# A post-norm block on one Trainium2 core: first values and one head's exponentials issued in pieces, and another order at the end

## The chip, the cores and the metric

The kernel runs on one core of a Trainium2 chip. The metric is the device time of one execution in microseconds (us); a time for a kernel is the median of its runs. Profiles are of one execution each, with their own time.

The engines are named as in the profile: PE (TensorE, matrix products; PEld is its loading of weights), DVE (VectorE), ACT (ScalarE), POOL (GpSimd) and SP (SyncE, which here only issues DMAs).

## The reference

The input x has 32 sequences of 512 tokens with 256 features. There are 16 heads of 16 features. Each sequence goes through a double causal attention, a residual and a layer norm; then the 512 tokens of the first sequence go through a mixture of 8 experts (the router's choices and weights cover 512 tokens), and everything is normed a second time. Cut to what matters:

```python
qk = x @ W_attn + b_attn                      # q and k; the values are x itself
y  = causal_attn(q, k, v)                     # first attention, softmax over keys
e  = v[:, :, 1:] - y[:, :, :-1]               # what the first one missed, one token on
k2 = x[:, :-1] @ W_k2 + b_k2
y2 = causal_attn(q[:, :, 1:], k2, e)          # second attention, with a zero row in front
x  = layernorm(x + proj(y) + proj(y2))
x  = layernorm(x + experts(x))                # in the kernel: experts for sequence 0 only
```

## The kernel before, in words

**Groups and steps.** A group is 4 heads of one sequence; there are 32 x 4 = 128 groups (`n_all`). `step(n)` runs for n = 0 to 131. In one step the kernel works on several groups at once: the maxima of group n, the exponentials of groups n - 1 and n - 2, the values (products of probabilities and values) of group n - 2, and the projections for groups to come. A step has five **slots** (`slot(n, u)`, u = 0 to 4), each followed by a **gap**, whose work stands in a list `rest[u]`. `add(gap, f, ...)` appends to such a list; some calls insert at its head. The order on PE, SP, DVE and POOL is the order of the Python calls; ACT's order is the scheduler's.

**A slot** makes scores twice: `maxima` (L271) multiplies queries and keys to find each row's maximum (PE products L301 and a mask L286, then DVE's `tensor_reduce`, L325), and `scores` (L356) makes the turned scores, minus the maximum (PE, L372), takes the exponential on ACT (L384) and sets what lies above the diagonal to zero on POOL (L388). Both are done for two pairs of heads; pair 1's scores are issued first, then pair 0's. Each head of a pair has its own PSUM bank. The tile of a slot has one or two **parts**, listed in `banks` (L348): slots 0 and 2 have parts of 384 and 128 columns, slot 3 has two of 256, slots 1 and 4 have one of 512. A part is three products for each head: two for queries and keys, and one for the maxima (`m_t`, `minus`).

**PSUM.** `pair_of_banks` (two buffers of two banks) holds the maxima's scores; `bank` (L81, four buffers of one bank) serves everything else: the turned scores (four for each slot), projections (`pj`), values (`av`), transposes (`yt`), the output projection (`po`), the experts. A product that takes a new buffer waits until the buffer taken four allocations earlier has been read.

**Values.** `values(n, a, lo, hi)` (L428) multiplies probabilities `pt` and values: `v_pad` for the first attention (a = 0), `e_pad` for the second (a = 1). Each product fills 32 rows for one of 4 heads, over the columns from its key block on. A copy by ACT (L450) takes the result to SBUF (`avs`). For a = 0 it is one call over 512 columns, in gap 1; for a = 1 there are two calls, columns 0 to 255 in gap 3 and 256 to 511 in gap 4. `normalize` (L499) turns the first attention's result on PE (`yt`), divides it and makes `e_pad` on DVE and POOL.

**Sums.** Two groups share a tile (`packed[two]`). `gather` (L452) sends softmax sums to DRAM and numerators to a packed tile; `narrow` (L464) loads the sums of both attentions back as 128 x 64, `inverse` (L469) inverts them on DVE, `unload` (L474) writes them to DRAM, `widen` (L479) loads them spread over the heads' rows (two DMAs of 256 KB), `weigh` (L487) multiplies (DVE, L490), and `unite` (L492) adds the two attentions on POOL (L497) into `ysT`. For the last two groups `narrow` to `unite` stand in step 130, and `attended` in step 131.

**Output.** `attended` (L543) makes four blocks of 128 tokens: products with W_proj (`po`, L551), the residual's addition on DVE (L554), then `twice_normed` (L560) with statistics (L566, L567). `scaled` (L573) makes the factor on POOL (L577, L578) and applies it: on POOL for most sequences, on DVE for the last one, followed by the store. For sequences 1 to 30 `scaled` is issued one gap after `attended`; for the last sequence `twice_normed` calls it at once, for each block.

Of the kernel before, what the change touches and what calls it, by code (L numbers as in the profile page):

```python
# [9 lines left out]
F32 = mybir.dt.float32  # L10
# [3 lines left out]
AF = mybir.ActivationFunctionType  # L14
# [3 lines left out]
P = 128  # L18
HD = 16
HS = 32  # L20
GH = 4
NH2 = 2
RUN = 64
# [12 lines left out]
def half(ap):  # L36
    return ap.bitcast(F32R)
# [3 lines left out]
def block_kernel(  # L41
# [16 lines left out]
    nc = tc.nc  # L58
    B, T, C = x.shape
    NB = T // P  # L60
    NC = C // P
# [10 lines left out]
    work = ctx.enter_context(tc.tile_pool(name="work", bufs=2))  # L72
    small = ctx.enter_context(tc.tile_pool(name="small", bufs=4))
    psum = ctx.enter_context(tc.tile_pool(name="psum", bufs=1, space=bass.MemoryType.PSUM))
    dram = ctx.enter_context(tc.tile_pool(name="dram", bufs=2, space=bass.MemoryType.DRAM))
# [13 lines left out]
    seqs = {}  # L89
# [109 lines left out]
    packed = {}  # L199
    moments = {}  # L200
# [155 lines left out]
    def scores(n, u, pair):  # L356
        parts = [p for p in banks[u] if 0 <= n - p[3] < n_all]
        if not parts:
            return [], lambda: None
        ps = [bank(f"sc{n}_{u}_{pair}_{hh}") for hh in range(NH2)]  # L360
        pt = work.tile([P, NH2, T], F32, tag=f"pt{u}", name=f"pt{n}_{u}_{pair}", bufs=2)
        todo = []


        def score(d, a, j, at, k, hh, rows):
            keys = minus[a][rows] if k == 2 else d["kk"][rows, a, j * P : (j + 1) * P]
            queries = d["q"][rows, k, j * P :] if k < 2 else d["m"][rows]
            to = ps[hh][:, at * P : at * P + T - j * P]
            if k == 2:
                queries = queries.rearrange("p (r i q) -> p i r q", r=GH, i=NB)[:, j:]  # L370
                to = to.rearrange("p (i r q) -> p i r q", r=GH, q=HS)
            nc.tensor.matmul(to, half(keys), half(queries), start=(k == 0), stop=(k == 2))  # L372

        for a, j, at, lag in parts:
            d = groups[n - lag]
            d["pt", a, j, pair] = pt[:, :, at * P : at * P + T - j * P]
            for k in range(3):
                todo.append((T - j * P, partial(score, d, a, j, at, k)))

        def exponentials():  # L380
            lo = parts[0][2] * P
            hi = parts[-1][2] * P + T - parts[-1][1] * P
            for hh in range(NH2):
                nc.scalar.activation(pt[:, hh, lo:hi], ps[hh][:, lo:hi], AF.Exp, scale=HD**-0.5)  # L384

            for a, j, at, _ in parts:
                diag = pt[:, :, at * P : (at + 1) * P]
                nc.gpsimd.affine_select(  # L388
                    diag, diag, pattern=[[0, NH2], [1, P]], compare_op=ALU.is_ge, fill=0.0, base=-a,
                    channel_multiplier=-1,  # L390
                )

        return todo, exponentials
# [34 lines left out]
    def values(n, a, lo=0, hi=T):  # L428
        b, g = divmod(n, NG)
        d = groups[n]  # L430
        vals = (v_pad, e_pad)[a]

        def first_of(g, h):
            return (g // 2 * GH + h) * WIDE + 2 * (g % 2)

        ps = bank(f"av{n}_{a}_{lo}")
        order = [j for j in ([0, 2, 1, 3] if a == 0 else [0, 1, 3, 2]) if j * P < hi]
        for j in order:
            first = max(lo, j * P)
            for h in range(GH):  # L440
                nc.tensor.matmul(  # L441
                    ps[HS * h : HS * (h + 1), first - lo : hi - lo],
                    vals[:, j, first_of(g, h) : first_of(g, h) + HS],
                    d["pt", a, j, h // NH2][:, h % NH2, first - j * P : hi - j * P],
                    start=(j == order[0]),
                    stop=(j == order[-1]),
                )
        if lo == 0:
            d["avs", a] = work.tile([P, T], F32, tag="avs", name=f"avs{n}_{a}")
        nc.scalar.copy(d["avs", a][:, lo:hi], ps[:, 0 : hi - lo])  # L450

# [9 lines left out]
        nc.sync.dma_start(p["sums"][a, k], avs[(HS - 1) * k :: HS])  # L461
        nc.sync.dma_start(p[a][GH * HD * k : GH * HD * (k + 1)], avs[1 - k :: 2])

    def narrow(two):  # L464
        p = packed[two]
        t = p["den"] = small.tile([P, RUN], F32, tag="den", name=f"den{two}", bufs=1)
        nc.sync.dma_start(t, p["sums"].rearrange("a k h (c q) -> (a k h c) q", q=RUN))

    def inverse(two):  # L469
        t = packed[two]["den"]  # L470
        nc.vector.tensor_scalar_max(t, t, 1e-30)
        nc.vector.reciprocal(t, t)

    def unload(two):  # L474
        p = packed[two]
        p["inv"] = dram.tile([2, 2, GH, T], F32, tag="inv", name=f"inv{two}")
        nc.sync.dma_start(p["inv"].rearrange("a k h (c q) -> (a k h c) q", q=RUN), p["den"])

    def widen(two):  # L479
        p = packed[two]  # L480
        r = p["r"] = work.tile([P, 2, T], F32, tag="r", name=f"r{two}", bufs=1)
        for a in range(2):
            nc.sync.dma_start(
                r[:, a], p["inv"][a].rearrange("k h t -> (k h) t").unsqueeze(1).to_broadcast([2 * GH, HD, T])
            )

    def weigh(two):  # L487
        p = packed[two]
        for a in range(2):
            nc.vector.tensor_mul(p[a], p[a], p["r"][:, a])  # L490

    def unite(two):  # L492
        b, c = divmod(two, NC)
        p = packed.pop(two)
        if c == 0:
            seqs[b]["ysT"] = work.tile([P, NC, T], F32, tag="ysT", name=f"ysT{b}", bufs=2)
        nc.gpsimd.tensor_add(seqs[b]["ysT"][:, c], p[0], p[1])  # L497

    def normalize(n):  # L499
        b, g = divmod(n, NG)  # L500
# [59 lines left out]
    def twice_normed(b, i):  # L560


        t = seqs[b]["h"]
        mv = small.tile([P, 2], F32, tag="mv2", name=f"mv{b}_{i}")
        stats = small.tile([P, nc.vector.BN_STATS_DIM], F32, tag="stats", name=f"st{b}_{i}")
        nc.vector.bn_stats(stats, t[:, i])  # L566
        nc.vector.bn_aggr(mv, stats)  # L567
        if b == B - 1:
            scaled(b, i, mv)
        else:  # L570
            moments[b, i] = mv

    def scaled(b, i, mv=None):  # L573
        t = seqs[b]["h"]
        mv = mv or moments.pop((b, i))
        r = small.tile([P, 1], F32, tag="r2", name=f"r{b}_{i}")
        nc.gpsimd.tensor_scalar(r, mv[:, 1:2], 1.0 + EPS, EPS * EPS, ALU.mult, ALU.add)  # L577
        nc.gpsimd.tensor_tensor(r, r, mhalf[:, 0:1], ALU.pow)  # L578

        by = nc.vector if b == B - 1 else nc.gpsimd  # L580
        by.tensor_scalar(t[:, i], t[:, i], mv[:, 0:1], r, ALU.subtract, ALU.mult)  # L581
        if b == B - 1:
            nc.sync.dma_start(out[b, i * P : (i + 1) * P], t[:, i])
# [102 lines left out]
    n_all = B * NG  # L686
    first_expert = 2 * NG + 4

    def step(n):
        ready = lambda k: 0 <= k < n_all  # L690
        rest = [[] for _ in units]
        b, r = divmod(n, NG)
        two, odd = divmod(n, 2)
        ahead, behind = two + 1, two - 2
# [3 lines left out]
        def add(gap, f, *args):  # L698
            rest[gap].append(partial(f, *args))
# [3 lines left out]
        if ready(2 * ahead):  # L703
# [5 lines left out]
            else:  # L709
                add(0, project, ahead, 1, 0, T // 2)  # L710
                add(2, project, ahead, 1, T // 2)
                add(3, project, ahead, 0, 0, T // 2)
        if ready(2 * behind) and not odd:
            add(0, narrow, behind)
        if ready(2 * two) and two and not odd:
            add(0, spread, two, 0, 1)
        if ready(n - 2):
            soon = n > n_all
            add(0 if soon else 1, values, n - 2, 0)
            add(0 if soon else 1, gather, n - 2, 0)  # L720
            rest[1 if soon else 2].insert(0, partial(normalize, n - 2))
            add(3, values, n - 2, 1, 0, T // 2)
            add(4, values, n - 2, 1, T // 2)
        if ready(2 * ahead) and odd:
            add(1, spread, ahead, 1, 1)
            add(2, spread, ahead, 0, 0)
            add(4, spread, ahead, 2, 0)
        if ready(2 * behind) and not odd:
            add(2, inverse, behind)
            add(3, unload, behind)  # L730
            add(4, widen, behind)
            if n > n_all + 1:
                add(4, weigh, behind)
                add(4, unite, behind)
        if ready(2 * behind) and odd and n < n_all + 2:
            add(1, weigh, behind)
            add(3, unite, behind)
# [11 lines left out]
        for b in range(B):  # L749
            end = (b + 1) * NG - 1  # L750
            last = b == B - 1
            for i in range(NB):
                if n == (end + 4 if last else min(end + 5 + i, n_all)):
                    add(0, attended, b, i)
                    if 0 < b < B - 1:
                        add(1, scaled, b, i)
            if n == end + 2:
                add(2, load_residual, b)
            for part in range(2):
                if n == (end + 3 if last else min(end + 3 + 2 * part, n_all - 1)):  # L760
                    add(3, biased, b, part)
            if 0 < b < B - 1 and n == min(end + 9, n_all + 2):
                rest[1].append(lambda b=b: store(b))
# [117 lines left out]
```

## Time and profile before

| | us |
|---|---|
| median of 3 runs | 2552.66 (2551.92 to 2559.37) |
| the profiled execution: time | 2553.1 |
| its span, first to last instruction | 2551.4 |
| PE busy | 2416.2 |
| DVE busy | 2034.4 |
| POOL busy | 1751.4 |
| ACT busy | 1660.6 |
| exponentials (L384), 2564 instructions | 1323.2 |
| first values' products (L441, v_pad), 4096 | 303.9 |
| second values' products (L441, e_pad), 6144 | 335.0 |
| one step in the middle, from one first-values block to the next | 18.2 |

The granted TensorE clock was 0.983 of full speed over the span. An instruction's row gives the start, the duration, engine, line, operation, and out<-in by the program's names; in brackets stands the idle time ahead of it and what ended it. Matmuls overlap, and PE's products of different rows run side by side, so durations of single products do not add up; starts are the safer reading.

### The profile page before, as it was taken

How to read it: one execution, taken by the hardware profiler on the slowest of the kernel's cores; microseconds unless marked ns; L12 is line 12 of the kernel's file. 1: busy time of each engine (PE TensorE's matmuls, PEld its weight loads, DVE VectorE, ACT ScalarE, POOL GpSimd, SP SyncE). 2: the span in 40 equal slices, each digit the busy share in tenths (PEclk: the TensorE clock that was granted, in tenths of full speed). 3: DMA queues.
4: the chain of work that ended last, by engine and by line, in shares of the span. 5: the costliest groups of instructions: out<-in, count | busy, mean ns of one | idle time of the engine just before them, and what ended most of it. 6: DMA issues, size and time to landing. Idle time of an engine off the chain costs nothing. (4 is left out here: it accounts for less than half of the span.)

```text
span 2551.4 us, 87424 instructions
## 1 busy us (share of the span) xinstructions
PE 2416.2 (95%) x35080; PEld 1735.8 (68%) x35080; DVE 2034.4 (80%) x3227; ACT 1660.6 (65%) x3350; POOL 1751.4 (69%) x3254
## 2 busy tenths in 40 slices
PE   7999999999999999999999999999999999999995
PEld 4766666677667667677776777677766767777763
DVE  6878777788888878888887888888887888888881
ACT  2766444476666667676766767667666667767662
POOL 4655555577777767777776777677776777777774
PEclk7999999999999999999999999999999999999997
DMA  5445433354545445445554545445454545445431
GB/s 136 109 111 134 112 100 107 96 134 125 131 133 130 120 120 129 134 131 134 132 138 106 133 125 132 132 128 139 111 132 125 135 129 134 128 115 133 127 102 60
DMA packets 262660, 314.04 MB, mean 123 GB/s; under 512 B 83064, under 2 KB 152688, under 8 KB 262256
## 3 DMA queue, kind: packets, MB, share of 16 engines
q1 hardware_dynamic: 259824, 308.01, 45.7%
q8 instruction: 278, 4.55, 0.8%
q14 instruction: 126, 1.03, 0.1%
q10 hardware_dynamic: 2368, 0.42, 0.1%
q0 software_dynamic: 64, 0.02, 0.0%
HBM read 115.26 MB, written 25.17 MB: 55 GB/s over the span
## 5 line engine op out<-in xcount | busy, mean ns | idle before, releaser
L325 DVE TENSOR_REDUCE top<-sm 128x2 f32<-128x1024 f32 (+4 forms) x1802 | 1529.4, 901 | 314.2 <-PE sc L372 189.1
L384 ACT ACTIVATE pt<-sc 128x512 f32<-128x512 f32 (+1 forms) x2564 | 1323.2, 603 | 441.2 <-PE sc L372 412.9
L388 POOL TENSOR_SCALAR_AFFINE_SELECT pt<-pt 128x256 f32<-128x256 f32 x2048 | 793.0, 409 | 636.4 <-ACT pt L384 627.4
L301 PE MATMUL sm<-kk_t,q_t 32*128 32x512 f32 (+2 forms) x7168 | 1031.1, 379 | 22.5 <-DMA kk_t<-pk 9.7
L372 PE MATMUL sc<-q_t,kk_t 32*128 32x256 f32 (+3 forms) x8192 | 993.0, 336 | 6.1 <-ACT pk L240 4.3
L372 PEld LDWEIGHTS sc<-q_t,kk_t 32*128 32x128 f32 x8192 | 646.8, 184 | 202.3 <-ACT pt L384 87.8
L372 PE MATMUL sc<-m_t,minus 32*128 32x256 f32 (+3 forms) x4096 | 694.7, 319 | 0.3
L301 PEld LDWEIGHTS sm<-kk_t,q_t 32*128 32x128 f32 x7168 | 611.1, 190 | 32.8 <-issue 18.3
L228 PE MATMUL pj<-xT,wq_sb 128*128 128x256 f32 (+1 forms) x1524 | 437.9, 411 | 44.7 <-DMA xT<-in_xT 9.3
L372 PEld LDWEIGHTS sc<-m_t,minus 32*128 32x128 f32 x4096 | 433.9, 185 | 12.4 <-issue 1.3
L228 PEld LDWEIGHTS pj<-xT,wq_sb 128*128 128x128 f32 x1524 | 264.1, 192 | 131.7 <-ACT pt L384 81.3
L441 PE MATMUL av<-pt,e_pad 128*32 128x256 f32 (+1 forms) x6144 | 335.0, 352 | 14.3 <-POOL e_pad L513 6.3
L450 ACT COPY avs<-av 128x256 f32<-128x256 f32 (+1 forms) x384 | 170.3, 444 | 265.6 <-issue 169.4
L286 PE MATMUL sm<-hide,pick 32*128 32x256 bf16 (+1 forms) x2560 | 337.0, 258 | 0.0
L441 PE MATMUL av<-pt,v_pad 128*32 128x512 f32 (+3 forms) x4096 | 303.9, 436 | 19.9 <-ACT pt L384 19.2
L441 PEld LDWEIGHTS av<-pt,e_pad 128*32 128x32 f32 x6144 | 170.0, 110 | 164.4 <-issue 46.0
L240 ACT ACTIVATE pk<-pj,bp_qk 128x256 f32<-128x256 f32 (+1 forms) x381 | 185.8, 488 | 129.5 <-PE pj L228 90.0
L441 PEld LDWEIGHTS av<-pt,v_pad 128*32 128x32 f32 x4096 | 142.0, 110 | 187.0 <-issue 160.6
L246 POOL TENSOR_TENSOR pk<-pk,lead 128x512 fp32r<-128x512 f32 x192 | 244.8, 1275 | 16.6 <-ACT lead L245 0.8
L581 POOL TENSOR_SCALAR h<-h,mv,r 128x256 f32<-128x256 f32 x120 | 147.0, 1225 | 13.1
L551 PE MATMUL po<-wp_sb,ysT 128*128 128x256 f32 x512 | 135.3, 390 | 12.7 <-POOL ysT L497 12.3
L243 POOL CAST lead<-pk 128x512 fp32r<-128x512 f32 x189 | 115.4, 611 | 28.5 <-ACT pk L240 26.8
(84 smaller groups left out, 1559.3 us busy)
## 6 DMA issues: line engine op xcount, KB each, us to landing
q_t<-lead SPq DMA_DIRECT2D x256, 128.0 KB
q_t<-pk SPq DMA_DIRECT2D x256, 128.0 KB
kk_t<-lead SPq DMA_DIRECT2D x256, 128.0 KB
kk_t<-pk SPq DMA_DIRECT2D x256, 128.0 KB
num<-avs SPq DMA_DIRECT2D x256, 128.0 KB
r<-inv SPq DMA_DIRECT2D x128, 256.0 KB
xT<-in_xT SPq DMA_DIRECT2D x32, 512.0 KB
x<-in_x SPq DMA_DIRECT2D x32, 512.0 KB
```

The lines of the kernel that those rows point to most:

```text
L228: nc.tensor.matmul(ps[:, 0 : hi - lo], wq_sb[:, m, c, part * P : (part + 1) * P], seqs[b]["xT"][:, c, lo:hi], start=(c == 0), stop=(c == N ...
L240: nc.scalar.activation(pk[:, lo:hi], ps[:, 0 : hi - lo], AF.Identity, bias=bp_qk[:, m, part : part + 1])
L246: nc.gpsimd.tensor_sub(half(pk), pk, lead)
L286: nc.tensor.matmul(ps[hh][:, 0 if alone else hh].rearrange("p (k c) -> p k c", c=P)[:, first::step], pick[rows], hide[rows, kinds[0] : kin ...
L301: nc.tensor.matmul(part(ps[hh], i, na, at)[:, 0 if alone else hh], half(d["q"][rows, k, i * P : (i + 1) * P]), half(d["kk"][rows, a : a + ...
L325: nc.vector.tensor_reduce(to, view, AX.X, ALU.max)
L372: nc.tensor.matmul(to, half(keys), half(queries), start=(k == 0), stop=(k == 2))
L384: nc.scalar.activation(pt[:, hh, lo:hi], ps[hh][:, lo:hi], AF.Exp, scale=HD**-0.5)
L388: nc.gpsimd.affine_select(diag, diag, pattern=[[0, NH2], [1, P]], compare_op=ALU.is_ge, fill=0.0, base=-a, channel_multiplier=-1,)
L441: nc.tensor.matmul(ps[HS * h : HS * (h + 1), first - lo : hi - lo], vals[:, j, first_of(g, h) : first_of(g, h) + HS], d["pt", a, j, h // N ...
L450: nc.scalar.copy(d["avs", a][:, lo:hi], ps[:, 0 : hi - lo])
L581: by.tensor_scalar(t[:, i], t[:, i], mv[:, 0:1], r, ALU.subtract, ALU.mult)
```

## The change

Three edits:

1. In `exponentials`, the exponential of pair 1's first head is issued once for each part of the tile instead of once for the whole tile. The other three heads' stay whole.
2. The first values (a = 0) are two calls, columns 256 to 511 first and then 0 to 255, in the same gap. `avs` is allocated by whichever comes first.
3. The end. `narrow`, `inverse`, `unload`, `widen` and `weigh` take a list of attentions. For the last two groups the first attention's half runs in gap 2 of step 129, and the second's, with `unite`, in gap 2 of step 130. The last `unite` is on DVE. The last sequence's four blocks are all added first (gap 0 of step 131), and scaled in the next gap.

```diff
         def exponentials():
-            lo = parts[0][2] * P
-            hi = parts[-1][2] * P + T - parts[-1][1] * P
+            runs = [(at * P, at * P + T - j * P) for _, j, at, _ in parts]
             for hh in range(NH2):
-                nc.scalar.activation(pt[:, hh, lo:hi], ps[hh][:, lo:hi], AF.Exp, scale=HD**-0.5)
+                for lo, hi in runs if pair and not hh else [(runs[0][0], runs[-1][1])]:
+                    nc.scalar.activation(pt[:, hh, lo:hi], ps[hh][:, lo:hi], AF.Exp, scale=HD**-0.5)
...
-        if lo == 0:
+        if ("avs", a) not in d:
             d["avs", a] = work.tile([P, T], F32, tag="avs", name=f"avs{n}_{a}")
...
-    def narrow(two):
+    def narrow(two, which=range(2)):
         p = packed[two]
-        t = p["den"] = small.tile([P, RUN], F32, tag="den", name=f"den{two}", bufs=1)
-        nc.sync.dma_start(t, p["sums"].rearrange("a k h (c q) -> (a k h c) q", q=RUN))
+        if "den" not in p:
+            p["den"] = small.tile([P, RUN], F32, tag="den", name=f"den{two}", bufs=1)
+        nc.sync.dma_start(p["den"][of(which)], flat(p["sums"], which))
...
-        nc.gpsimd.tensor_add(seqs[b]["ysT"][:, c], p[0], p[1])
+        by = nc.vector if b == B - 1 and c == NC - 1 else nc.gpsimd
+        by.tensor_add(seqs[b]["ysT"][:, c], p[0], p[1])
...
         nc.vector.bn_aggr(mv, stats)
-        if b == B - 1:
-            scaled(b, i, mv)
-        else:
-            moments[b, i] = mv
+        moments[b, i] = mv
...
-        if ready(2 * behind) and not odd:
+        if n >= n_all + 1:
+            one = [n - n_all - 1]
+            if one[0] < 2:
+                for f in (narrow, inverse, unload, widen, weigh):
+                    add(2, f, n_all // 2 - 1, one)
+            if one[0] == 1:
+                add(2, unite, n_all // 2 - 1)
+        elif ready(2 * behind) and not odd:
             add(0, narrow, behind)
...
-            add(0 if soon else 1, values, n - 2, 0)
+            for half_of in (T // 2, 0):
+                add(0 if soon else 1, values, n - 2, 0, half_of, half_of + T // 2)
...
-        if ready(2 * behind) and not odd:
+        if ready(2 * behind) and not odd and n <= n_all:
             add(2, inverse, behind)
             add(3, unload, behind)
             add(4, widen, behind)
-            if n > n_all + 1:
-                add(4, weigh, behind)
-                add(4, unite, behind)
...
                     add(0, attended, b, i)
-                    if 0 < b < B - 1:
+                    if b:
                         add(1, scaled, b, i)
```

`inverse`, `unload`, `widen` and `weigh` are changed as `narrow` is: they work on the chosen attentions' 64 rows of `den`, or on the chosen attention's half of `r`.

More of the change, by code (lines that the diff above doesn't have):

```diff
@@ L462, in gather, with of, flat, inverse @@
         nc.sync.dma_start(p[a][GH * HD * k : GH * HD * (k + 1)], avs[1 - k :: 2])
-    def narrow(two):
-        p = packed[two]
-        t = p["den"] = small.tile([P, RUN], F32, tag="den", name=f"den{two}", bufs=1)
-        nc.sync.dma_start(t, p["sums"].rearrange("a k h (c q) -> (a k h c) q", q=RUN))
-    def inverse(two):
-        t = packed[two]["den"]
+    def of(which):
+        return slice(64 * which[0], 64 * (which[-1] + 1))
+    def flat(t, which):
+        return t[which[0] : which[-1] + 1].rearrange("a k h (c q) -> (a k h c) q", q=RUN)
+    def narrow(two, which=range(2)):
+        p = packed[two]
+        if "den" not in p:
+            p["den"] = small.tile([P, RUN], F32, tag="den", name=f"den{two}", bufs=1)
+        nc.sync.dma_start(p["den"][of(which)], flat(p["sums"], which))
+    def inverse(two, which=range(2)):
+        t = packed[two]["den"][of(which)]
         nc.vector.tensor_scalar_max(t, t, 1e-30)
         nc.vector.reciprocal(t, t)
-    def unload(two):
+    def unload(two, which=range(2)):
         p = packed[two]
-        p["inv"] = dram.tile([2, 2, GH, T], F32, tag="inv", name=f"inv{two}")
-        nc.sync.dma_start(p["inv"].rearrange("a k h (c q) -> (a k h c) q", q=RUN), p["den"])
-    def widen(two):
+        if "inv" not in p:
+            p["inv"] = dram.tile([2, 2, GH, T], F32, tag="inv", name=f"inv{two}")
+        nc.sync.dma_start(flat(p["inv"], which), p["den"][of(which)])
+    def widen(two, which=range(2)):
         p = packed[two]
-        r = p["r"] = work.tile([P, 2, T], F32, tag="r", name=f"r{two}", bufs=1)
-        for a in range(2):
+        if "r" not in p:
+            p["r"] = work.tile([P, 2, T], F32, tag="r", name=f"r{two}", bufs=1)
+        for a in which:
             nc.sync.dma_start(
-                r[:, a], p["inv"][a].rearrange("k h t -> (k h) t").unsqueeze(1).to_broadcast([2 * GH, HD, T])
+                p["r"][:, a], p["inv"][a].rearrange("k h t -> (k h) t").unsqueeze(1).to_broadcast([2 * GH, HD, T])
             )
-    def weigh(two):
+    def weigh(two, which=range(2)):
         p = packed[two]
-        for a in range(2):
+        for a in which:
             nc.vector.tensor_mul(p[a], p[a], p["r"][:, a])
@@ L567, in twice_normed, with scaled @@
         nc.vector.bn_aggr(mv, stats)
-        if b == B - 1:
-            scaled(b, i, mv)
-        else:
-            moments[b, i] = mv
-    def scaled(b, i, mv=None):
+        moments[b, i] = mv
+    def scaled(b, i):
         t = seqs[b]["h"]
-        mv = mv or moments.pop((b, i))
+        mv = moments.pop((b, i))
         r = small.tile([P, 1], F32, tag="r2", name=f"r{b}_{i}")
```

## The prediction

> **What bounds the kernel now.** I read the page first (busy shares), then the list of waits, then the timeline of one step in the steady part, and last the chain of waits at the end.
>
> ```profile
> PE 2416.2 (95%) x35080; PEld 1735.8 (68%) x35080; DVE 2034.4 (80%) x3227; ACT 1660.6 (65%) x3350; POOL 1751.4 (69%) x3254
> ```
>
> TensorE is busy 95% of the span, so it looks like the bound, and ScalarE at 65% looks free. The waits qualify this. Three of their lines:
>
> ```profile
> PEld pj L228 <- ACT pt L384: 81.3, 229, 1.4
> ...
> PE av L441 <- ACT pt L384: 19.2, 111, 0.3
> ...
> PE sm L301 <- DVE top L325: 8.5, 8, 3.2
> ```
>
> In 229 places the weights of the next projection wait for an exponential (L384); waits for VectorE's maxima are rare. The timeline of one step shows why. First ScalarE, then TensorE, at the end of the score slots 0, 2 and 3 of one step; each line is the first exponential of a slot, or the first product after the slot (start, duration).
>
> ```profile
> 1505.34 0.60 ACT L384 ACTIVATE pt<-sc 128x512 f32<-128x512 f32 x1 [0.68 <-PE sc L372]
> ```
> ```profile
> 1505.99 0.48 PE L228 MATMUL pj<-xT,wq_sb 128*128 128x256 f32 x1
> ```
> ```profile
> 1513.19 0.60 ACT L384 ACTIVATE pt<-sc 128x512 f32<-128x512 f32 x1 [0.43 <-POOL r L578]
> ```
> ```profile
> 1513.84 0.33 PE L504 MATMUL yt<-ident,avs 128*128 128x128 f32 x1
> ```
> ```profile
> 1516.49 0.60 ACT L384 ACTIVATE pt<-sc 128x512 f32<-128x512 f32 x1 [0.52 <-PE sc L372]
> ```
> ```profile
> 1517.14 0.48 PE L228 MATMUL pj<-xT,wq_sb 128*128 128x256 f32 x1
> ```
>
> Start to start each pair is 0.65 us: 0.60 us of exponential, then 0.05 us until TensorE goes on. The four "one" banks explain it: a slot takes all four, in the order pair 1 head 0, pair 1 head 1, pair 0 head 0, pair 0 head 1; the next product needs the bank taken four allocations earlier, that of pair 1 head 0, and that is free when its exponential ends. Reading every such turn in the trace, 353 of 378 turns after slots 0, 2 and 3 start 0.04 to 0.07 us after that exponential's end. So there is a closed chain: product of pair 1 head 0, its exponential, next product. ScalarE is 35% idle, and still the first exponential of a slot sets the pace. What lengthens it lengthens the kernel.
>
> **The exponentials in pieces.** The change cuts just that exponential, where its tile has two parts: slots 0 and 2 into 384 and 128 columns, slot 3 into 256 and 256. That adds 383 instructions. It could gain only if the first piece started before the second part's products. The built program of the changed kernel says it does not: the first piece waits for the count on TensorE which that head's very last product (128 columns of m_t) reaches; none of its 384-column products raises the count, and the second piece has no wait of its own:
>
> ```
> L384 Activation pt59_2_1_24329<-sc59_2_1_0_24327 128x384 [waits PE_49,Activation_49,Pool_49]
> L384 Activation pt59_2_1_24329<-sc59_2_1_0_24327 128x128
> L384 Activation pt59_2_1_24329<-sc59_2_1_1_24328 128x512 [waits PE_49]
> ```
>
> Dependencies are kept by bank, not by columns. The release of the bank goes with the second piece. So both pieces start when the whole one did, and the end moves by what cutting costs. Nearest rows: two 256-column exponentials back to back near the end.
>
> ```profile
> 2519.58 0.38 ACT L384 ACTIVATE pt<-sc 128x256 f32<-128x256 f32 x1 [0.34 <-PE sc L372]
> ```
> ```profile
> 2519.86 0.38 ACT L384 ACTIVATE pt<-sc 128x256 f32<-128x256 f32 x1
> ```
>
> First start to last end is 0.66 us, against 0.60 for one of 512: 0.06 us more for a cut. For 384+128 no row exists; four of 512 take 2.07 us in a row, so a whole one adds 0.49 us to a run; 0.49 less 0.43 (512 columns at the 0.83 ns that separates 0.60 from 0.38 over 256 columns) leaves the same 0.06 per extra instruction. Cost: 353 x 0.061 = **+21.5 us**. Bounds: zero (the next instruction wholly overlapped) and 0.17 us (no overlap: 2 x 0.38 - 0.60), that is 0 to +60 us; I take the measured pair.
>
> The Trainium skill, PSUM — Partial Sum Buffer, section "PSUM bank collisions raise a hardware error", wants semaphores by bank and quadrant, not by address, since two engines on one bank collide even in disjoint columns; that speaks against this edit, and agrees with the wait above. The trace cannot show a collision. ScalarE: Activation LUTs, section "What ACT_TABLE_LOAD costs", gives 186 ns + 0.833 ns a column and about 93 ns overlap, so an estimated 93 ns per cut, +33 us in all; the trace has 0.06, and decides.
>
> **First values in halves.** Instead of one group of 16 products of 512, 256, 384 and 128 columns come 16 for the right half and 8 for the left; columns are equal (1280 a head). The second values (e_pad) already have this form. Their two blocks and the first values' one, from the timeline, with the first score product after each:
>
> ```profile
> 1509.71 2.36 PE L441 MATMUL av<-pt,v_pad 128*32 128x512 f32 x32 [0.16 <-ACT pt L384]
> 1512.00 0.44 PE L372 MATMUL sc<-q_t,kk_t 32*128 32x384 f32 x2
> ```
> ```profile
> 1518.20 0.86 PE L441 MATMUL av<-pt,e_pad 128*32 128x256 f32 x16
> 1518.99 0.50 PE L372 MATMUL sc<-q_t,kk_t 32*128 32x512 f32 x2
> ```
>
> Start to start: 2.29 us whole; 0.79 for the left half, 1.65 for the right (1502.50 to 1504.15), 2.44 together. The 0.15 difference is one more change between kinds of products; back to back in one place only the streaming is paid (single groups of four: 0.43 us for 512 columns, 0.215 for 256). I take 0.01 us, 128 x 0.01 = **+1.3 us**; bounds 0 and 128 x 0.15 = 19 us. The 0.16 us stall ahead stays: it is slot 1's exponential, which has one part and is not cut. The copy to SBUF (0.59 us, one) becomes two of 0.37; the second ends about 0.2 us earlier after the last product. That helps slot 2's last bank, whose products are some 0.15 us late now, but the turn after slot 2 follows the exponential (1513.19 + 0.60 + 0.05 = 1513.84), so it gives nothing. ScalarE's 35% idle hides the extra copy.
>
> **The end.** Its chain of waits, from the moment the inverted sums are loaded back:
>
> ```profile
> 2530.33 0.62 SPq L483
> ...
> 2530.99 4.37 DMA r<-inv
> ...
> 2535.49 0.70 DVE num L490
> 2536.19 0.07 issue
> 2536.26 1.27 POOL ysT L497
> 2537.53 0.04 issue
> 2537.57 1.24 PE po L551 x2
> ...
> 2548.00 0.41 DVE h L581
> ```
>
> Now the first attention's half is done a step sooner, beside the e_pad products of 2519.7 to 2524.2. Loading the sums, the reciprocal, the store and the widening took 9.2 us at the end of before (2524.64 to 2533.82); from 2513.65, where the first sums leave, that is over by 2523: hidden. One widening DMA instead of two is left: the first of the two freed its product at 2533.82, the second at 2535.49, so -1.7. The addition runs on VectorE (0.72 for this shape at L490) instead of GpSimd (1.27 and a hand-over): -0.6. On SP the store of sequence 30 (512 KB) now stands ahead of the sums' load, at about 2525.8 instead of 2526.71: its packets last some 1.5 us, so I charge +0.5. xr's load stands behind the first widening, at about 2520.5, needed by 2535: free. ysT comes 1.8 us sooner.
>
> Then the four blocks. Before, each runs add, statistics, GpSimd's power and scaling in series: 2538.83 to 2548.41 is 9.6 us. After, the adds of all come first. TensorE delivers the last block 4.3 us after the first; add, statistics and aggregate 1.1, power 0.9, last scaling 0.4 and a queue of earlier ones 0.3: 7.0 us. That is -2.6. Together **-4.4 us** (-2.5 to -5.5).
>
> **Sum.** +21.5 + 1.3 - 4.4 = +18.4 us on the profiled span of 2551.4: 2569.8, with 1.7 around it 2571.5. That run (2553.1) is 0.4 over the median, 2552.66, so I say **2571 us**, 0.7% slower.
>
> **Rivals.**
> 1. Give-back: the 25 turns that wait for something else (xT loads, about every 74 us) swallow part, or a cut costs 0.03. Then +10 + 1 - 4.4: about 2559.
> 2. The other side, the copy's relief counts: slot 2's end follows its late products, not the exponential, and each step gains 0.17 there: -22, total 2549. For: slot 2 lasts 1.88 us (1512.00 to 1513.88), slot 0 with the same shapes 1.71 (1504.15 to 1505.86). Against: 117 of 119 turns after slot 2 follow the exponential. It decides from the point where the relief exceeds the 0.18 us added to a step.
> 3. It does as meant: the first piece starts early, and turns follow TensorE's last products, which end at 1505.86, 1513.71 (without the late copy) and 1517.08 where the turns come at 1505.99, 1513.84 and 1517.14: 0.32 us a step, 118 steps, -38: about 2512. Against: the program's waits.
> 4. A cut costs 0.1 us (+35), or the halves the e_pad rate (+21.5 + 19), less 4.4: 2585 to 2589.
>
> **Chances.** Forecast (2562 to 2582) 0.69; rival 1 0.09; rival 2 0.07; rival 3 0.05; rival 4 0.10. What can be told from no change is about 0.3%, 7.7 us. Slower: 0.69 + 0.10 and a little of rival 1, 0.80; within: 0.15; faster: 0.05. The range 2553 to 2589 takes in rivals 1 and 4 and leaves out rivals 2 and 3; the far bounds of a cut, 0 and 0.17 us (2549 and 2609), lie outside, because two rows of this trace give 0.06.
>
> **What would show it.** Right: in slots 0, 2 and 3 the first piece starts with its wait on the last score product, the turn comes about 0.71 us after the first piece's start instead of 0.65; slots 1 and 4 keep 0.65 (first values 0.74); step length grows by about 0.18 us everywhere; the v_pad block keeps 2.3 us; the last scaling ends 7 us after the first block's add begins. Wrong: first pieces that start while TensorE writes the second part, turns that no longer follow the exponential, or a v_pad block of 2.4 us.

## The result and the profile after

The changed kernel takes **2564.06 us** (median of 13 runs, 2557.89 to 2568.88); the kernel before took 2551.64 us beside it (13 runs, 2540.38 to 2559.37). The ratio is 1.0052 [1.0038, 1.0066], 13 us more. The forecast was 2571 us, 18 more. The profiled execution of after has a span of 2557.9 us and a time of 2559.6, near the low end of its runs, so its span says less than the ratio. Ratios leave out two executions that ran at a granted clock of 0.60 and 0.75 (one of e4_no_pieces, one of g2_spread_first_halves).

The busy shares of the page, and two of the waits shown of before:

```profile
PE 2401.1 (94%) x37128; PEld 1763.3 (69%) x37128; DVE 2038.6 (80%) x3230; ACT 1705.0 (67%) x3861; POOL 1748.9 (68%) x3253
```
```profile
PEld pj L228 <- ACT pt L384: 94.8, 230, 1.4
...
PE sm L301 <- DVE top L325: 8.1, 9, 3.2
```

230 turns (229 before) wait for the exponential, now 94.8 us in all instead of 81.3. The pair of the first step shown of before, in the timeline of after: the first piece, then both pieces as one group, and the product that follows.

```profile
1508.78 0.49 ACT L384 ACTIVATE pt<-sc 128x384 f32<-128x384 f32 x1 [0.68 <-PE sc L372]
```
```profile
1508.78 0.66 ACT L384 ACTIVATE pt<-sc 128x384 f32<-128x384 f32 x2 [0.68 <-PE sc L372]
```
```profile
1509.49 0.48 PE L228 MATMUL pj<-xT,wq_sb 128*128 128x256 f32 x1 [0.18 <-ACT pt L384]
```

The first piece starts with its wait on the last score product, both pieces last 0.66 us where the whole lasted 0.60, and TensorE goes on 0.71 us after the first piece's start instead of 0.65. So far every step of the forecast is there.

One thing is not: the first values after slot 1. Two steps of after, first exponential and first product:

```profile
1512.48 0.60 ACT L384 ACTIVATE pt<-sc 128x512 f32<-128x512 f32 x1 [1.22 <-PE sc L372]
```
```profile
1513.13 0.64 PE L441 MATMUL av<-pt,v_pad 128*32 128x256 f32 x8
```
```profile
1530.79 0.60 ACT L384 ACTIVATE pt<-sc 128x512 f32<-128x512 f32 x1 [1.22 <-PE sc L372]
```
```profile
1531.53 0.42 PE L441 MATMUL av<-pt,v_pad 128*32 128x256 f32 x4 [0.18 <-ACT pt L384]
```

The lower pair keeps the 0.74 us of before. The upper one takes 0.65. The right half is issued first; in half of the steps its first product waits for the bank alone and no longer for GpSimd too, and it starts 0.09 us sooner. The forecast did not see this.

The measure that the rest of the work turned on is the length of a step, from one first-values block to the next, over the 104 steps of the middle: its median is the undisturbed step, its mean has the stalls in it.

| profiled execution | median step | mean step | span |
|---|---|---|---|
| before | 18.20 | 18.54 | 2551.4 |
| after | 18.39 | 18.62 | 2557.9 |

The undisturbed step grew by 0.19 us, as forecast (0.18), or by 0.15 on average, since it is 18.30 in the two steps of four where the first values start sooner. The mean grew by 0.08, about half of that. Most of the difference lies in TensorE's clock: four of the 104 steps of before (21.09 to 23.32 us long) and two of after (22.84 and 21.76) have a stretch of 3.4 us in which the granted clock is half of full speed. One of before: a product that waits for `kk_t`, then the stretch (start and end, length, busy us of PE, PEld, DVE, ACT and POOL, then the granted clock, here 0.50, the DMA share and GB/s).

```profile
1605.19 0.50 PE L301 MATMUL sm<-kk_t,q_t 32*128 32x512 f32 x2 [1.14 <-DMA kk_t<-pk]
```
```profile
1606.80:1610.20 3.40, 3.38 (x16) 2.49 (x16) 3.03 (x6) 1.96 (x5) 2.27 (x5) 0.50 0.33 73
```

Without these steps the means are 18.41 and 18.55, 0.14 us apart, as the undisturbed steps say. In the 104 middle steps of the 14 profiles of this case there are 57 such stretches; each began within 5 us after TensorE had started to stand idle for at least 0.6 us. Not every idle time of that length was followed by one.

### The profile page after: what moved, and what is told of

The parts are those of the page before. It is cut to its first block, busy times and chain, and to the rows that moved or that the text cites. A ratio compares the mean times of both kernels' runs of the same rounds, so it can differ in the third digit from the quotient of the medians.

```text
span 2557.9 us, 92303 instructions
## 1 busy us (share of the span) xinstructions
PE 2401.1 (94%) x37128; PEld 1763.3 (69%) x37128; DVE 2038.6 (80%) x3230; ACT 1705.0 (67%) x3861; POOL 1748.9 (68%) x3253
## 5 line engine op out<-in xcount | busy, mean ns | idle before, releaser
L384 ACT ACTIVATE pt<-sc 128x512 f32<-128x512 f32 (+3 forms) x2947 | 1347.5, 550 | 470.8 <-PE sc L372 449.9
L372 PE MATMUL sc<-q_t,kk_t 32*128 32x384 f32 (+3 forms) x8192 | 960.4, 333 | 3.2 <-ACT pk L240 2.2
L372 PEld LDWEIGHTS sc<-q_t,kk_t 32*128 32x128 f32 x8192 | 600.7, 184 | 199.8 <-ACT pt L384 88.2
L372 PE MATMUL sc<-m_t,minus 32*128 32x256 f32 (+3 forms) x4096 | 670.0, 319 | 0.3 <-issue 0.2
L372 PEld LDWEIGHTS sc<-m_t,minus 32*128 32x128 f32 x4096 | 390.5, 185 | 11.8 <-issue 0.8
L228 PEld LDWEIGHTS pj<-xT,wq_sb 128*128 128x128 f32 x1524 | 264.8, 192 | 145.2 <-ACT pt L384 94.8
L450 ACT COPY avs<-av 128x256 f32<-128x256 f32 x512 | 190.9, 373 | 209.3 <-PE av L441 102.6
L441 PE MATMUL av<-pt,v_pad 128*32 128x256 f32 (+1 forms) x6144 | 306.4, 347 | 16.9 <-ACT pt L384 11.4
L441 PEld LDWEIGHTS av<-pt,v_pad 128*32 128x32 f32 x6144 | 196.1, 110 | 130.0 <-ACT pt L384 25.6
```

What stands on the lines that cost most here:

```text
L228: nc.tensor.matmul(ps[:, 0 : hi - lo], wq_sb[:, m, c, part * P : (part + 1) * P], seqs[b]["xT"][:, c, lo:hi], start=(c == 0), stop=(c == N ...
L441: nc.tensor.matmul(ps[HS * h : HS * (h + 1), first - lo : hi - lo], vals[:, j, first_of(g, h) : first_of(g, h) + HS], d["pt", a, j, h // N ...
```

## The experiments

### One edit at a time

The first edit alone, the second alone, the third alone, and the second and third together (diffs against before; the third is the change's lines on `narrow` to `unite`, `scaled` and their places in `step`).

```diff
 e1_pieces
+                for lo, hi in runs if pair and not hh else [(runs[0][0], runs[-1][1])]:
 e2_halves
-            add(0 if soon else 1, values, n - 2, 0)
+            for half_of in (T // 2, 0):
+                add(0 if soon else 1, values, n - 2, 0, half_of, half_of + T // 2)
 e3_end
+        if n >= n_all + 1:
+            one = [n - n_all - 1]
...
+                for f in (narrow, inverse, unload, widen, weigh):
+                    add(2, f, n_all // 2 - 1, one)
 e4_no_pieces
 (e2_halves and e3_end)
```

> The kernel before with the first exponential of slots 0, 2 and 3 in pieces and nothing else. Theory (a cut lengthens the chain product, exponential, next product): each turn after slots 0, 2 and 3 comes 0.06 us later, 353 turns, +18 to +23 us, ratio 1.007 to 1.009; slots 1 and 4 keep their turns of 0.65 us. Rival (the cut is hidden, ScalarE being 35% idle, and the slowdown of the whole change is from the halves): within 4 us of before. Rival (first pieces start early): faster by 30 us or more.

> The kernel before with the first values in two halves, right half first, and nothing else. Theory now (as the trace of the changed kernel suggests): the halves stream as fast as the whole, and in half of the steps the first product waits for the bank alone and starts 0.05 instead of 0.145 us after the exponential: 64 x 0.09 = 6 us, less about 1, so -2 to -7 us. My forecast had +1. Rival (a second block costs what e_pad's does): +19. Rival (the earlier copy relieves slot 2's end): -22.

> The kernel before with the new end and nothing else. Theory: the four blocks' part is shorter by 2.6 us, the inverted sums by 0.7, together about -3 us, all of it after the last exponential; the steady part is unchanged. Forecast had -4.4. Rival (the store ahead of the sums' load eats the gain): 0.

> The changed kernel with whole exponentials again. Theory: the halves' -5 and the end's -3 remain, -6 to -10 us against before, ratio 0.996 to 0.998, and about 20 us faster than the changed kernel: faster than both. Rival (the pieces are not what costs): stays near the changed kernel, +12.

| run | median us | ratio to before | in us |
|---|---|---|---|
| e1_pieces | 2563.24 | 1.0034 [1.0019, 1.0050] | +8.7 |
| e2_halves | 2563.26 | 1.0029 [1.0012, 1.0045] | +7.4 |
| e3_end | 2555.40 | 0.9995 [0.9978, 1.0012] | -1 |
| e4_no_pieces | 2558.42 | 1.0020 [0.9997, 1.0043] | +5 |

The parts add up: 0.34 + 0.29 - 0.05 = 0.58%, against 0.52% for the whole change. But each of the two edits in the steady part misses its expectation: the pieces cost 9 us, not 18 to 23, and the halves cost 7 where they should have gained. e4_no_pieces misses too: it is 8 us below the changed kernel, not 20, and not faster than before. The undisturbed step is as the theory said with the pieces, 18.40 (18.20 before). With the halves the median, 18.21, hides it: steps there that nothing held up took 18.10 to 18.12 us or 18.19. So I looked at the stalls. TensorE's waits for transfers between 524 and 2450 us (engine and line, what it waited for: us in total, times, longest), before, then with the halves, then with the pieces:

```profile
PE pj L228 <- DMA xT<-in_xT: 8.4, 11, 1.2
...
PE sm L301 <- DMA kk_t<-pk: 2.7, 4, 1.1
PE sm L301 <- DMA q_t<-pk: 1.0, 3, 0.5
```
```profile
PE pj L228 <- DMA xT<-in_xT: 14.1, 16, 1.4
...
PE sm L301 <- DMA kk_t<-pk: 5.7, 8, 1.0
...
PE sm L301 <- DMA q_t<-pk: 2.5, 5, 0.7
PE sc L372 <- DMA m_t<-turned: 2.3, 7, 0.5
```
```profile
PE pj L228 <- DMA xT<-in_xT: 10.8, 11, 1.7
...
PE sm L301 <- DMA kk_t<-pk: 1.1, 1, 1.1
PE sm L301 <- DMA q_t<-pk: 0.8, 3, 0.3
```

12.1 us before, 24.6 with the halves, 12.7 with the pieces: the halves double these waits, the pieces take none away. All four transfers are issued by SyncE, so I looked at its queue. One stretch of before (start, duration of the issue, count):

```profile
1579.93 0.40 SPq L338 DMA_DIRECT2D turned<-tr  x1
1580.42 0.55 SPq L461 DMA_DIRECT2D sums<-avs  x1
1581.02 0.52 SPq L462 DMA_DIRECT2D num<-avs  x1
1584.47 2.27 SPq L346 DMA_DIRECT2D m_t<-turned  x4
1587.16 0.52 SPq L259 DMA_DIRECT2D kk_t<-lead  x1
```

One issue takes 0.4 to 0.6 us, a step has some twenty of them (12.4 us of a step's mean 18.54), and they leave in order. The four loads of `m_t` need what `turned` wrote to DRAM, so the queue stands still from 1581.54 to 1584.47 until that has landed. Its waits in before (524 to 2450 us):

```profile
SPq L346 <- DMA turned<-tr: 330.7, 103, 6.1
...
SPq L338 <- DVE tr L336: 34.8, 39, 3.2
```

331 us, 3.2 at a time, for the landing; only 35 us for VectorE's `tr`, a wait that shows that the queue has time to spare. From `turned` to the next `turned` there are therefore a landing, some twenty issues, in every second step one more landing (`r <- inv` waits for `inv`, 113 us in 52 times), and some 2 us a step for everything else: a **second closed chain**, nearly as long as the step, beside the one of TensorE and the exponential. The theory from here on: when TensorE's chain gets shorter, as with the halves, the queue falls behind and TensorE waits for transfers; when it gets longer, as with the pieces, the queue catches up and stalls go away. The rival is that the edits have costs of their own on TensorE and ScalarE. For the halves the waits above bear the theory out, and the queue's wait for `tr` is down to 16.9 us. For the pieces they do not: TensorE's waits for transfers stay, and so do the queue's for `tr` (39.5 us) and `turned` (331.3).

The Trainium skill, DMA: Bandwidth & Descriptors, section "Issuing engines are not separate DMA queues", says that the sequencer's time to start a DMA is usually small beside the DMA itself. For one transfer this trace agrees: `turned` above took 0.40 us to issue and 4.54 until `m_t` could leave. In one queue the issues add up all the same, 2.27 us for the four of `m_t` alone.

### The left half first

The second edit with its two calls in the other order:

```diff
-            for half_of in (T // 2, 0):
+            for half_of in (0, T // 2):
```

> The second edit alone with the left half of the columns first, so that the first half's first product always reads masked probabilities and waits for GpSimd as before. SP-chain theory: TensorE's start after the exponential stays at 0.145 us in all steps instead of 0.053 in half of them, it doesn't run ahead of SyncE, and the cost falls from 7 us to 0 to 4 us above before. Rival (the second set of products, or the two copies, cost): 6 us or more above before, as with the right half first.

2558.50 us, ratio 1.0006 [0.9991, 1.0021], with before at 2557.49 beside it. The same products and copies in another order cost nothing that can be measured, and the waits for transfers are 17.0 us, between 12.1 and 24.6. That speaks for the theory, though the distance to e2_halves (0.0023, each interval about 0.0016 to either side) is only just resolved.

### The queue in another order

```diff
-        if ready(n - 1):
-            add(0, augment, n - 1)
...
         if ready(2 * two) and two and not odd:
             add(0, spread, two, 0, 1)
...
-        if r == 1 and b + 1 < B:
-            add(2, load, b + 1)
+        if r == 1 and b + 1 < B:
+            add(0, load, b + 1)
+        if ready(n - 1):
+            add(0, augment, n - 1)
```

This is f1_queue; f2_queue_halves and f3_queue_pieces add the second and the first edit to it.

> The kernel before with SyncE's queue reordered and nothing else: in the first gap of every step the four row-maxima loads (m_t <- turned), which wait for a transfer to land, are issued behind the gap's other issues instead of ahead of them, and the next sequence's loads of xT and x go out two gaps sooner. SP-chain theory (the in-order queue, with that landing in it, is a second chain of nearly the step's own length): 1.1 to 2.7 us of slack per step on SP, TensorE's waits for xT, kk_t, q_t and m_t (12 us in 524 to 2450 us in the profile of before) fall under 4 us, time 5 to 15 us below before. Rival (those waits are only part of what would be late anyway): within 4 us of before.

> The reordered queue together with the first values in halves (second edit alone, which by itself cost about 7 us). SP-chain theory: with the queue out of the way the halves show what the regular step says, about 0.09 us less in half of the 128 steps, so 2 to 7 us below the reordered queue alone. Rival (the halves cost TensorE or ScalarE something of their own): 5 to 9 us above the reordered queue alone.

> The reordered queue together with the exponentials in pieces (first edit alone, which by itself cost about 9 us where 21 us were forecast). SP-chain theory: the part given back in transfers is not there to give back any more, so 15 to 22 us above the reordered queue alone. Rival (the pieces' turns cost less than the regular step says, whatever the queue does): 6 to 11 us above the reordered queue alone.

f1_queue took 2619.66 us, ratio 1.0240 [1.0212, 1.0267]: 61 us **slower**, where 5 to 15 less were expected. Of TensorE's waits for transfers one line is left; those for xT, kk_t and q_t are gone as expected:

```profile
PE sc L372 <- DMA m_t<-turned: 54.4, 29, 3.5
```

SyncE's timeline ahead of one of these stalls:

```profile
1406.99 0.54 SPq L338 DMA_DIRECT2D turned<-tr  x1
1407.63 0.92 SPq L461 DMA_DIRECT2D sums<-avs  x1
1408.60 0.60 SPq L462 DMA_DIRECT2D num<-avs  x1
1412.75 0.35 SPq L467 DMA_DIRECT2D den<-sums  x1
1413.20 1.12 SPq L257 DMA_DIRECT2D q_t<-lead  x2
1414.41 1.19 SPq L257 DMA_DIRECT2D q_t<-pk  x2
1415.69 2.29 SPq L346 DMA_DIRECT2D m_t<-turned  x4
```

`den <- sums` also waits for a landing, that of `sums` issued just before: the queue stood until 1412.75, with `m_t` now behind it, 8.70 us after `turned` instead of 4.54. I had put one landing behind another. Three steps of four were at 18.20 to 18.21 us, the fourth at 21.75.

The waits are only part of the 61 us. The end of the stall that follows the lines above, and the stretch after it, at half the full clock:

```profile
1419.68 0.58 PE L372 MATMUL sc<-m_t,minus 32*128 32x256 f32 x2 [2.10 <-DMA m_t<-turned]
```
```profile
1419.40:1426.20 6.80, 6.52 (x60) 4.35 (x62) 2.45 (x2) 3.01 (x6) 3.63 (x6) 0.50 0.53 155
```

Such stretches last 75 us in all over the 104 middle steps of f1_queue, against 14 in before, an estimated 31 us of lost clock (half of the difference). The waits for transfers are 42 us more (54.4 less 12.1). Together the two cover the slowdown.

f2_queue_halves: 2607.17 us, 1.0196 [1.0171, 1.0221], 11 us below f1_queue by the ratios; f3_queue_pieces: 2628.98 us, 1.0284 [1.0261, 1.0308], 11 us above. The halves had changed sign, as the theory said. The pieces had not reached the 15 to 22 us, but with a stall of this size in one step of four (its step fell from 21.75 to 20.76 under the pieces) the run could not decide that. The granted clock differs too: 0.9745 on average over the runs of f3_queue_pieces, 0.971 over those of f1_queue, an estimated 9 us less lost.

### The spreads first, then the row maxima, then the sums

The same with `narrow` behind `augment`, so that only issues that wait for little stand in the time of the landing:

```diff
 (f1_queue, and)
-        if ready(2 * behind) and not odd:
-            add(0, narrow, behind)
         if ready(2 * two) and two and not odd:
             add(0, spread, two, 0, 1)
         if r == 1 and b + 1 < B:
             add(0, load, b + 1)
         if ready(n - 1):
             add(0, augment, n - 1)
+        if ready(2 * behind) and not odd:
+            add(0, narrow, behind)
```

g1_spread_first is before with this order, g2_spread_first_halves has the second edit too, g3_spread_first_pieces the first, g4_spread_first_halves_end the second and third.

> The kernel before with its SyncE queue reordered in another way than in the run f1_queue, where the row-maxima loads stood behind den <- sums, which waited up to 3.8 us for the sums to land, and TensorE then waited 1.9 us for m_t at one step in four (54 us in all). Here the order of the first gap is: the spreads of q_t or kk_t, the next sequence's xT and x, the four row-maxima loads, and only then den <- sums. SP-chain theory: no waits for xT, kk_t, q_t of more than 0.25 us, those for m_t gone, every step near 18.20 us, time 8 to 25 us below before. Rival (what the waits took shows up as another wait): within 4 us of before or slower.

> That order of the queue together with the first values in halves, the right half first. SP-chain theory: steps of 18.12 us in half of the steps as in f2_queue_halves, so 3 to 12 us below g1_spread_first (f2_queue_halves stood 12 us below f1_queue). Rival (the 7 us that the halves cost by themselves are TensorE's or ScalarE's own): 5 to 9 us above g1_spread_first.

> The queue's order of g1_spread_first together with the exponentials in pieces (first edit). SP-chain theory: nothing late in the queue takes any of the pieces' lead back, so the forecast's term shows: 353 turns of 0.058 to 0.065 us, 15 to 23 us above g1_spread_first (whose ratio to before was 0.9921), so 0.998 to 1.001 of before. Rival (the pieces cost about 9 us whatever the queue does, as in f3_queue_pieces against f1_queue): 6 to 12 us above, 0.9945 to 0.997 of before.

> That order of the queue with the second and the third edit, and exponentials whole: the version that the runs so far point to. The halves gave 8 us there, and the end is 2.6 to 3.1 us shorter in the trace of after: 0 to 4 us below g2_spread_first_halves (0.9889 of before), so 0.987 to 0.989 of before. Rival (the end's steps are hidden or give back, as the end alone showed no difference that could be measured): 0.989 or above.

| run | median us | before beside it | ratio to before |
|---|---|---|---|
| g1_spread_first | 2529.81 | 2548.97 | 0.9921 [0.9904, 0.9937] |
| g2_spread_first_halves | 2521.91 | 2548.97 | 0.9889 [0.9869, 0.9908] |
| g3_spread_first_pieces | 2548.32 | 2555.98 | 0.9971 [0.9957, 0.9985] |
| g4_spread_first_halves_end | 2518.07 | 2555.98 | 0.9861 [0.9840, 0.9882] |

The order of one queue alone is worth 20 us, with not one instruction more or less. The stretch of g1_spread_first that answers to the one shown of before:

```profile
1560.27 1.33 SPq L483 DMA_DIRECT2D r<-inv  x2
1565.56 0.32 SPq L338 DMA_DIRECT2D turned<-tr  x1
1565.98 0.55 SPq L461 DMA_DIRECT2D sums<-avs  x1
1566.58 0.52 SPq L462 DMA_DIRECT2D num<-avs  x1
1567.20 0.53 SPq L259 DMA_DIRECT2D kk_t<-lead  x1
1567.82 0.54 SPq L259 DMA_DIRECT2D kk_t<-pk  x1
1568.46 2.30 SPq L346 DMA_DIRECT2D m_t<-turned  x4
```

The two issues of `kk_t` fill the landing, and the queue now stands still ahead of `turned` (1561.60 to 1565.56), where it waits for VectorE. Its waits and TensorE's for transfers say the same over 524 to 2450 us:

```profile
SPq L338 <- DVE tr L336: 183.3, 93, 3.9
...
SPq L346 <- DMA turned<-tr: 3.7, 5, 1.3
```
```profile
PE sc L372 <- DMA m_t<-turned: 4.3, 10, 0.6
```

331 us of waiting for `turned` have become 3.7, and 12.1 us of TensorE's waits 4.3. These 8 us are less than the 20 that the time fell by. In the profiles the mean step fell by 0.22 us, 24 us over the 104 steps; 15 us of that lie in the four steps of before with a stretch at half the clock, and g1_spread_first has none. Steps, as in the table above:

| profiled execution | median step | mean step | mean without steps at half clock |
|---|---|---|---|
| before | 18.20 | 18.54 | 18.41 |
| e1_pieces | 18.40 | 18.60 | 18.60 (it has none) |
| g1_spread_first | 18.20 | 18.32 | 18.32 (none) |
| g3_spread_first_pieces | 18.39 | 18.53 | 18.53 (none) |

The cut costs the undisturbed step the same with both queues (0.20 and 0.19 us). The means differ by 0.06 us with the old queue and by 0.22 with the new one, which looks as if the old queue gave something back. But the four steps of before at half clock make that difference: without them the old queue has 0.19. The profiled e1_pieces is also the fastest of its 12 executions, at their highest clock (0.988). Nor do the times show a give-back: the pieces cost 8.7 us in the old order (4 to either side) and 0.9971 / 0.9921 = 0.50%, 12.9 us, in the new one (some 5.5 to either side). These two cannot be told apart, and the second lies between its two expectations. Both are less than the 21.5 us that the steps say; why, these runs do not show.

The halves cost 7.4 us in the old order and save 0.9889 / 0.9921 = 0.32%, 8 us (some 6.5 to either side), in the new one. So their cost hangs on the queue's order, and not on products or copies of their own. Why the waits outweigh the earlier start in the old order, so that a gain becomes a loss, is not shown. How much of the 8 us is the earlier start of half of the first values is not settled: 0.09 us in 64 steps make 6; the mean step fell by 0.02, or by 0.09 without the two steps of g2_spread_first_halves at half clock; and the first twenty steps of these two executions differ by 7 by themselves.

g4_spread_first_halves_end beats both kernels: 36 us below before by the ratio (1.39%). Against g2_spread_first_halves its 0.28% less has an interval that includes zero.

## Why the prediction was right, and where it was not

The sign and the range held: 2564 us lies in 2553 to 2589, 7 below the forecast. That it came so near is in part luck: against the single edits, the forecast had the pieces 13 us too dear, the halves 6 us too cheap and the end's gain 3 us too large, and these errors cancel in part. Step by step:

- **The closed chain of product, exponential, product**: right. The turns wait for the cut exponential as they did for the whole one, 0.06 us later.
- **No early start of the first piece** (rival 3): right, by the waits and by 0.71 us from its start to the turn.
- **The price of a cut**, 0.061 us from two rows of the tail: right, 0.66 against 0.60 us. The Trainium skill, ScalarE: Activation LUTs, section "What ACT_TABLE_LOAD costs", would have it at an estimated 93 ns; the trace shows 60.
- **353 turns make +21.5 us**: the failed step is the size of this term. The undisturbed step grew by what it says, but the kernel by 8.7 us (e1_pieces), and by 12.9 with the queue in another order. I had counted the 25 turns that wait for something else, and taken them for all that could give anything back. The price is near rival 1's (+10, given 0.09), but its reason does not show: the waits for xT are 10.8 us with the pieces and 8.4 before. That SyncE's queue catches up when TensorE's chain slows was my explanation, and the waits do not bear it out (12.7 us for transfers against 12.1). What takes up the rest of the 21.5 us stays open. My list of waits had none of SyncE's in it, and I had not looked at the granted clock in the long steps.
- **The halves, +1.3 us**: failed in size. The products did cost next to nothing, as the term says: with the left half first (e7_left_first) the undisturbed step is 18.21 us against 18.20. I missed that the right half's first product needs no wait for GpSimd in half of the steps (-0.09 us each), and that in this order of the queue the waits for transfers would grow: 24.6 us instead of 12.1, and 7.4 us more in all.
- **Copy's relief** (rival 2): did not show; turns after slot 2 still follow the exponential.
- **The end, -4.4 us**: right in sign by the trace, mis-sized; e3_end by itself shows -1 us, which its interval cannot tell from nothing. The chain of waits of after:

```profile
2535.39 0.57 SPq L593
...
2536.07 2.65 DMA den<-sums
...
2539.55 1.69 DMA inv<-den
2541.26 3.71 DMA r<-inv
...
2544.98 0.70 DVE num L499
...
2545.71 0.70 DVE ysT L507
```

From the end of the last copy to the end of `ysT` it is 12.2 us (2534.24 to 2546.41), against 12.9 before (2524.62 to 2537.53): -0.7, not -1.8. The widening (0.62 + 4.37 us before, 3.71 now) and the addition gave 1.3 and 0.7 as forecast or nearly; the loss is in `den <- sums`, 2.65 us against 1.64 with the 512 KB store just ahead of it, where I had charged 0.5, and in `inv <- den`, 1.69 against 1.43 (e3_end has 2.42 and 1.69). The four blocks: the first addition and the four scalings at the end, in the timeline of after.

```profile
2547.77 0.42 DVE L564 TENSOR_TENSOR h<-po,xr 128x256 f32<-128x256 f32 x1 [1.37 <-PE po L561]
```
```profile
2553.18 1.56 DVE L588 TENSOR_SCALAR h<-h,mv,r 128x256 f32<-128x256 f32 x4
```

2547.77 to 2554.74 is 6.97 us, forecast 7.0, against 9.6 before: right.

Left open: why the pieces cost 9 to 13 us where the steps say 21.5, whether the whole would show in a kernel whose queue never makes TensorE wait (g3_spread_first_pieces still waits 6.4 us for `m_t`), and by how much the halves gain there.

## What to carry to other kernels

Look for closed chains on every engine, the DMA-issuing one too: add up its issues and its landing waits over one step, and if that comes near the step's length, a gain elsewhere can turn into waits for transfers, as with the halves. Compare the median step with the mean step before pricing an edit by its count of places, and look at the granted clock in the steps that stand out before comparing means of two profiles. In an in-order queue, put an issue that waits for a landing behind the ones that wait for little, and not behind another such landing (here 61 us slower).

## What the hardware showed that I had not expected

- A transfer's landing depends on what was issued just ahead of it. `turned` (32 KB) took 4.54 us from issue to the `m_t` loads in before, where `m_t` waited for it; in g1_spread_first, where the queue had been idle for 4 us ahead of it, the loads went out 2.90 us after it and hardly ever waited (3.7 us in 524 to 2450). In before, `r <- inv` (512 KB) is the issue ahead of `turned` in 52 steps. Where `turned` followed within 2 us of that issue's start, `m_t` left 4.35 us after `turned` (median of 47); in the two steps where it followed after more than 3 us, 2.36 and 1.63.
- A product that waits for ScalarE and for GpSimd starts 0.74 us after the start of a 0.60 us exponential, even if GpSimd is done (in before its last work had ended at least 0.9 us earlier in all 104 steps); with the wait for ScalarE alone it is 0.65 us.
- A stall of TensorE can cost more than its own time. After the wait of 2.10 us in f1_queue the granted clock was 0.50 for 6.8 us, and the products of second values that took 0.86 us in before took 1.51.
